# The last batch of a perceiver block, finished by tiles of 128 latents

## The chip, the cores and the metric

The kernel runs on one core of a Trainium2 chip. Its time is the device time of one execution in microseconds; for each kernel the median of several runs is given. A profile is one further execution, recorded by the hardware profiler; its row times are in microseconds from its first instruction.

The core's engines are TensorE (PE in the profile; PEld is its weight load), VectorE (DVE), ScalarE (ACT), GpSimd (POOL) and SyncE (SP, here only for DMAs). Each works off its own queue in order. PE writes to PSUM, eight banks of 2 KB per partition; DVE and ACT read it.

## What is computed

One perceiver layer on four batches of 256 latents with 256 channels; each batch has a context of 4096 rows with 192 channels. All in float32.

```python
x = x + xattn(layernorm(x), ctx)   # 16 heads of 16; 256 queries, 4096 keys
x = x + attn(layernorm(x))         # causal, 16 heads; q and k normed by head
x = x + ffn(layernorm(x))
# ffn: h = gelu([x, slot mean] @ w1 + b1); logits = h @ w2 + b2, scaled by tau
#      alpha = softmax over the 8 largest of 64 logits
#      slots = GRU(alpha.T @ x / sum(alpha), slot_init); slots mix by an attention
#      y = layernorm(slots + mixed); out = alpha @ (y @ wvp + bvp) @ wo + bo
```

## The kernel before

**Cross-attention.** The context comes in chunks of 512 keys (8 per batch). `keys` (L74) and `values` (L101) make a chunk's keys `kt` (channels first) and values `v`, with a column of ones beside each head, so that weighing also gives the softmax denominators. An iteration of the main loop (L2150 on) takes two blocks of 128 keys against all 256 latents. `cross_block` (L1769) does the scores of one block: 8 matmuls of 512 columns (`scores`, L161; two heads by 256 latents, on four row groups of PE), and the exps on ACT into `prob`. `cross_weigh` and `weigh` (L170) multiply the exps with the values: 8 matmuls per block and half of the heads, 256 columns, four column groups of PE. `cross_add` (L1790) adds the result from PSUM to `sums` on DVE. So 16 iterations make a batch, and four batches one long stream.

**Order.** PE, DVE and ACT run in the order of the program text; no scheduler moves their instructions. The eight banks are four pairs, turned by one step with each iteration (L2156). An iteration is: scores of the first block, weighing of the *iteration before* (`behind`), scores of the second block, then planned extra work (`take`), then keys (even iterations) or values (odd ones) of the next chunk, which the iterations after it use.

**The other layers** of batch b are cut into steps, put by `plan` (L1684 to L1760) into the iterations of batch b+1: `cross_turn`, `att_turned`, `cross_out` (the output of cross-attention), `x1_turned`, `qk`, `self_values`, `qk_turned` (the input of self-attention), an iteration of self-attention, `self_out`, `x2_turned`, `hidden`, and for the slots `routing`, `slot_inputs`, `alpha_turned`, `gates` and on. The slots of two batches (0 and 1, 2 and 3) go together. `first_more` and `second_more` (L1749, L1753) stand in the last two iterations of the last batch: the slot values of batches 0 and 1, routing, slot inputs and alpha of batch 2, and `give` (L1653) for batches 0 and 1: two matmuls of alpha with the slot values, `x2` added on DVE, DMA to the output.

**The ending** (`ending`, L1886) is what the last batch has left when the stream ends, with nothing to lie beside: weighing of the last two blocks, turning and dividing (`turn`, L189), `channels_turned`, `project` by `wo`, norm, `qk_product`, `self_values`, `head_sums` and `head_root`, `qk_turned`, self-attention with `last_block` (8 exps), masks on DVE (`self_masks`), `self_weigh`, `project` by `awo`, norm, `w1`, Gelu, `routing`, slots of batches 2 and 3, outputs. Each step takes all 256 latents (two tiles of 128, t = 0 and 1). `fill` (L1055) puts idle matmuls of 0.43 us into PE's waits. `preload` (L944) has ACT load a function table early. `moments`, `rsqrt` (L925: by ACT's root and a reciprocal, or by ten steps on DVE) and `all_in_range` (L1662, a check of the denominators) are on DVE. `temp()` (L918) gives one of 8 scratch buffers in turn.

Of the kernel before, what the change touches and what calls it, by code (L numbers as in the profile page):

```python
# [900 lines left out]
def fast_(es, tc, nc, a, out, k, const, x0):  # L901
# [219 lines left out]
    def same_rows(col):  # L1121

        t = small.tile([P, P], F32, name="same", tag="same")
        nc.vector.tensor_copy(t, col.to_broadcast([P, P]))
        return t
# [27 lines left out]
    def set_norms(bank):  # L1153

        rep = small.tile([P, P], F32, name="same", tag="same")
# [235 lines left out]
    def self_out(s, bank):  # L1391
        for t in range(QT):
            product(
                bank[:, t * C : (t + 1) * C],
                lambda c: s.attT[:, c, t * P : (t + 1) * P],
                lambda c: awo[:, c, :],
            )
        s.x2 = held.tile([P, QT, C], F32, name="x2", tag="x2", bufs=3)
        nc.vector.tensor_tensor(s.x2, halves(bank), s.xo, ALU.add)
        yield  # L1400
        apply = norm(s.x2)
        yield
        yield
        s.x2n = held.tile([P, QT, C], F32, name="x2n", tag="x2n", bufs=1)
        apply(s.x2n)
        with_bias(s, "x2", s.x2, fbo)
# [8 lines left out]

    def routing(s, bank):

        for t in range(QT):
            nc.tensor.matmul(
                bank[:, t * SLOTS : (t + 1) * SLOTS],  # L1420
                s.hT[:, t * P : (t + 1) * P],
                w2,
                start=True,
                stop=True,
            )
        lg, rest, best, ex = (
            small.tile([P, QT, n], F32, name=name, tag=name, bufs=1)
            for name, n in (("lg", SLOTS), ("rest", SLOTS), ("best", 8), ("ex", SLOTS))
        )
        top, asum = (small.tile([P, QT], F32, name=name, tag=name) for name in ("top", "asum"))  # L1430
# [6 lines left out]
        yield  # L1437
        for t in range(QT):
# [45 lines left out]
    def alpha_turned(s, bank):  # L1484
# [5 lines left out]
        if s.b % 2 == 0:  # L1490
            s.two.alphaT = held.tile([P, NQ], F32, name="alphaT", tag="alphaT", bufs=1)
        nc.scalar.copy(s.two.alphaT[r], bank[r, 0:NQ])

    def gates(w, *room):

        r, z, n, keep = (
            small.tile([P, 2, S2], F32, name=f"gate_{x}", tag=f"gate_{x}", bufs=1) for x in "rznk"
# [143 lines left out]
    def given(s, t, dst, start=True):  # L1641
# [3 lines left out]
            dst, s.two.alphaT[r, t * P : (t + 1) * P], s.two.sv[r], start=start, stop=True  # L1645
# [7 lines left out]
    def give(s, bank):  # L1653
# [3 lines left out]
        nc.vector.tensor_tensor(res, halves(bank), s.x2, ALU.add)  # L1657
# [88 lines left out]

    def first_more(x_0, x_1, y_0, y_1):  # L1749
        slot_values(batches[0].two, x_1)  # L1750
        return routing(batches[B - 2], x_0)

    def second_more(x_0, x_1, y_0, y_1):  # L1753
        s = batches[B - 2]
        slot_inputs(s, x_0)
        alpha_turned(s, x_1)
        for e, bank in zip(batches, (y_0, y_1)):
            give(e, bank)

    plan[B - 1, 15, 5], plan[B - 1, 16, 5] = first_more, second_more  # L1760
# [107 lines left out]
    def last_block(s, c, pairs):  # L1868

        pr = {}  # L1870
        for (j, h), sc in zip(((1, 0), (1, 1), (0, 0), (0, 1)), pairs):
            n = 2 * NQ // (j + 1)
            pt = pr[j, h] = pp.tile([P, 2, 2 * NQ], F32, name="prob", tag="prob")
            for m in range(2):
                r = pair_rows(h, m)
                nc.tensor.matmul(
                    sc[:, m, 0:n],
                    s.sk[r, c, j * P : (j + 1) * P],
                    s.sq[r, c, :, j * P :],
                    start=True,  # L1880
                    stop=True,
                )
            nc.scalar.activation(pt[:, :, 0:n], sc[:, :, 0:n], AF.Exp)
        return pr

    def ending(blocks, *pairs):  # L1886
# [3 lines left out]
        both_ = s.two  # L1890
        (x_0, x_1), (y_0, y_1), (z_0, z_1), (w_0, w_1) = ([m[:, i, :] for i in range(2)] for m in pairs)

# [4 lines left out]
        def channels_turned(bank, src, c):  # L1897
            for t in range(QT):
                nc.tensor.transpose(
                    bank[:, t * P : (t + 1) * P], src[:, t, c * P : (c + 1) * P], ident  # L1900
                )

        def tokens_turned(bank, src, t):
            for c in range(2):
                nc.tensor.transpose(
                    bank[:, c * P : (c + 1) * P], src[:, t, c * P : (c + 1) * P], ident
                )

        def tokens(dst, bank, t, copy):
            copy(  # L1910
                dst[:, :, t * P : (t + 1) * P],
                bank[:, 0:C].rearrange("p (c q) -> p c q", c=2),
            )

        def turn_half(sums, which, c, bank):
            return turn(nc, k, small, sums[c], c, bank, dens[:, s.b, which, c], s.att)

        def project(weights, banks_, alone):
            for c in range(2):
                for t in range(QT):  # L1920
                    nc.tensor.matmul(
                        banks_[t][:, 0:C],
                        s.attT[:, c, t * P : (t + 1) * P],
                        weights[:, c, :],
                        start=(c == 0 and alone),
                        stop=(c == 1),
                    )


        cross_weigh(s, blocks, 0, y_0)  # L1930
        cross_add(s, 0, y_0)
        preload(AF.Sqrt)
        cross_weigh(s, blocks, 1, y_1)


        s.att = halves(temp())
        divide = turn_half(s.sums, 0, 0, z_0)
        cross_add(s, 1, y_1)
        divide()
        turn_half(s.sums, 0, 1, z_1)()  # L1940
        s.attT = halves(temp())
        channels_turned(w_0, s.att, 0)
        nc.scalar.copy(s.attT[:, 0, :], w_0[:, 0:NQ])
        fill(x_1, 0.43)
        channels_turned(w_1, s.att, 1)
        nc.vector.tensor_copy(s.attT[:, 1, :], w_1[:, 0:NQ])
        project(wo, (x_0, y_1), True)
        for t, bank in enumerate((x_0, y_1)):
            nc.vector.tensor_tensor(s.xo[:, t, :], bank[:, 0:C], s.xo[:, t, :], ALU.add)


        s.x1T = halves(temp())
        tokens_turned(z_0, s.xo, 0)
        tokens(s.x1T, z_0, 0, nc.vector.tensor_copy)
        tokens_turned(z_1, s.xo, 1)
        tokens(s.x1T, z_1, 1, nc.scalar.copy)
        s.qk = held.tile([P, QT, 2 * C], F32, name="qk", tag="qk", bufs=1)
        s.var = small.tile([P, QT * 2 * H], F32, name="var", tag="var")
        rs = small.tile([P, QT * 2 * H], F32, name="rs_h", tag="rs_h")
        s.eps = small.tile([P, QT], F32, name="epsx", tag="epsx")  # L1960
        s.rs1 = small.tile([P, QT], F32, name="rs1", tag="rs1")

        def qk_product(t, bank):
            product(
                bank,
                lambda c: s.x1T[:, c, t * P : (t + 1) * P],
                lambda c: wqkv[:, c, 0 : 2 * C],
# [286 lines left out]
```

## Time and profile before

| what | value |
|---|---|
| median of 3 runs | 848.32 us (848.3 to 848.55) |
| the profiled execution | 850.1 us, of which span 848.2 us |
| granted TensorE clock, mean | 0.995 |
| busy | PE 828.2, ACT 605.7, DVE 309.1, POOL 16.7 us |
| last four iterations, start of the first block's scores | 741.61, 752.15, 762.77, 772.48 us |
| last weighing, start | 785.00 us |
| logits of the last batch on DVE | 821.24 us |
| last DMA issue | 842.09 us |

How to read it. A row of the timeline is: start, duration, engine, line, operation, written tile, read tiles, shapes and count; a bracket at its end gives the engine's idle time before it, and what ended it. The ends of matmuls are modelled, starts are recorded; a matmul in float32 leaves two records. "32*128" before a shape is the part of the array used, rows by columns: four such matmuls run beside each other. The chain is what ended last, followed back from the end; "issue" is time with no wait that the profile shows. Lines are those of the kernel of that profile. A stretch's row gives its length, busy time of each engine with the number of instructions, granted clock (1.00 is full), DMA share and GB/s.

### The profile page before, as it was taken

To read this page: it belongs to the slowest core of one execution; us is meant where nothing else is said; L and a number is where in the kernel's file an instruction comes from. 1 tells how busy PE (TensorE), PEld (TensorE's weight loads), DVE (VectorE), ACT (ScalarE), POOL (GpSimd) and SP (SyncE) were. 2 spreads that over 40 slices of the span, in tenths; PEclk is the share of its full clock that TensorE was granted. 3 is DMA by queue.
4 is the path that set the end of the run, shared out by engine and by line. 5 is a ranking of instruction groups with operands and counts; after the bars stand their busy time and mean duration, and the time that the engine had idled before them with its cause. 6 is when DMAs were issued, how large, how long until landed. Compare 5 with 4: busy or idle time off the path is not lost.

```text
span 848.2 us, 18509 instructions
## 1 busy us (share of the span) xinstructions
PE 828.2 (98%) x7975; PEld 440.2 (52%) x7975; DVE 309.1 (36%) x760; ACT 605.7 (71%) x842; POOL 16.7 (2%) x20
## 2 busy tenths in 40 slices
PE   8999999999999999999999999999999999999885
PEld 5445455545555555545545555555545555445554
DVE  3124234232263352212253453332334433123663
ACT  4777776767677768777677767767768767877551
POOL 1000100000000010000000010000000000000000
PEclk9999999999999999999999999999999999999998
DMA  7600101000000000000000000000000000000000
GB/s 204 163 27 26 26 14 63 26 27 26 26 26 26 2 26 26 26 26 27 27 26 26 2 26 26 26 25 2 26 26 26 26 19 10 24 2 2 26 1 29
DMA packets 21817, 25.79 MB, mean 30 GB/s; under 512 B 6240, under 2 KB 13280, under 8 KB 21728
## 3 DMA queue, kind: packets, MB, share of 16 engines
q1 hardware_dynamic: 20784, 23.75, 9.8%
q8 instruction: 64, 1.05, 0.5%
q10 hardware_dynamic: 848, 0.79, 0.3%
q14 instruction: 25, 0.20, 0.1%
q0 software_dynamic: 96, 0.01, 0.0%
HBM read 23.48 MB, written 1.05 MB: 29 GB/s over the span
## 4 chain that ended last, share of the span: by engine, by line
PE 94%; ACT 2%; DVE 2%; issue 0%; ACTq 0%; DVEq 0%
PE banks L165 30%; PE banks L179 27%; PE banks L993 7%; PE banks L80 7%; PE banks L107 7%; PE banks L86 4%; PE banks L120 4%; PE banks L1845 1%; PE banks L981 1%; PE banks L194 1%; PE banks L1058 1%; ACT prob L1782 1%; PE banks L1814 1%; PE banks L1461 1%; ACT prob L1824 0%
## 5 line engine op out<-in xcount | busy, mean ns | idle before, releaser
L1782 ACT ACTIVATE prob<-banks 128x1024 f32<-128x1024 f32 x384 | 366.8, 1045 | 0.0
L165 PE MATMUL banks<-qh,kt 32*128 32x512 f32 x2048 | 267.7, 620 | 1.5 <-DVE qh L1036 1.2
L179 PE MATMUL banks<-prob,v 128*32 128x256 f32 x4096 | 234.3, 381 | 1.6 <-DVE tmp L1657 0.8
L1780 ACT ACTIVATE prob<-banks 128x512 f32<-128x512 f32 x256 | 138.9, 595 | 130.8 <-PE banks L165 130.5
L179 PEld LDWEIGHTS banks<-prob,v 128*32 128x32 f32 x4096 | 126.5, 110 | 125.7 <-ACT prob L1780 45.8
L165 PEld LDWEIGHTS banks<-qh,kt 32*128 32x128 f32 x2048 | 103.9, 183 | 119.2 <-issue 66.9
L1796 DVE TENSOR_TENSOR sums<-banks,sums 128x512 f32<-128x512 f32 x120 | 82.6, 690 | 194.3 <-PE banks L179 168.5
L107 PE MATMUL banks<-wv,ctx 128*128 128x256 f32 x256 | 61.6, 384 | 0.0
L80 PE MATMUL banks<-ctx,wk 128*128 128x512 f32 x128 | 61.5, 603 | 0.1
L107 PEld LDWEIGHTS banks<-wv,ctx 128*128 128x128 f32 x256 | 46.8, 190 | 14.7 <-ACT prob L1780 7.6
L150 DVE COPY v<-banks 128x512 f32<-128x512 f32 x35 | 23.9, 690 | 81.4 <-PE banks L120 81.4
L94 DVE TENSOR_SCALAR kt<-banks,bk 128x512 f32<-128x512 f32 x32 | 24.0, 750 | 66.9 <-PE banks L86 66.8
L150 ACT COPY v<-banks 128x512 f32<-128x512 f32 x29 | 17.0, 586 | 30.1 <-PE banks L120 28.8
L120 PE MATMUL banks<-wv,ctx 64*128 64x256 f32 x256 | 36.3, 402 | 0.0
L86 PE MATMUL banks<-ctx,wk 64*128 64x512 f32 x128 | 36.1, 641 | 0.0
L95 ACT ACTIVATE kt<-banks,bk 128x512 f32<-128x512 f32 x32 | 22.1, 689 | 18.0 <-PE banks L86 17.1
L80 PEld LDWEIGHTS banks<-ctx,wk 128*128 128x128 f32 x128 | 20.9, 189 | 21.6 <-ACT prob L1782 12.1
L120 PEld LDWEIGHTS banks<-wv,ctx 64*128 64x128 f32 x256 | 22.0, 186 | 11.1 <-issue 9.3
L1829 DVE TENSOR_TENSOR prob<-prob,tri 128x512 f32<-128x512 f32 x32 | 20.8, 688 | 10.5 <-ACT prob L1824 9.8
L987 DVE COPY tmp<-banks 128x512 f32<-128x512 f32 x17 | 11.7, 691 | 33.8 <-PE banks L981 33.8
L1824 ACT ACTIVATE prob<-banks 128x512 f32<-128x512 f32 (+1 forms) x30 | 17.9, 694 | 8.5 <-PE banks L1814 8.5
L993 PE MATMUL banks<-wqkv,tmp 128*128 128x512 f32 (+1 forms) x64 | 23.0, 497 | 0.7 <-ACT prob L1824 0.5
(276 smaller groups left out, 504.9 us busy)
## 6 DMA issues: line engine op xcount, KB each, us to landing
ctx<-in_ctxT SPq DMA_DIRECT2D x32, 256.0 KB, 3.1
ctx<-in_ctxT SPq DMA_DIRECT2D x64, 128.0 KB, 3.2
x<-in_x SPq DMA_DIRECT2D x4, 256.0 KB, 3.5
wih<-in_ffn_WihT SPq DMA_DIRECT2D x1, 768.0 KB, 7.9
tmp<-in_ffn_WhhT SPq DMA_DIRECT2D x3, 256.0 KB, 5.8
out<-tmp SPq DMA_DIRECT2D x3, 256.0 KB, 2.3
wq<-in_L_xattn_Wq ACTq DMA_DIRECT2D x1, 256.0 KB, 5.8
wo<-in_L_xattn_Wo SPq DMA_DIRECT2D x1, 256.0 KB, 5.1
```

The lines of the kernel that those rows point to most:

```text
L80: nc.tensor.matmul(pk[c], k.wk[:, 0, c * P : (c + 1) * P], cx[:, 0, :], start=True, stop=False)
L86: nc.tensor.matmul(pk[c], k.wk[left(c), 1, c * P : (c + 1) * P], cx[left(c), 1, :], start=False, stop=True,)
L94: nc.vector.tensor_scalar(kt[:, 0, :], pk[0], k.bk[:, 0:1], None, ALU.add)
L107: nc.tensor.matmul(pv[n // 2][:, n % 2, :], cx[:, 0, n * P : (n + 1) * P], k.wv[:, 0, :], start=(n % 2 == 0), stop=False, skip_group_check ...
L120: nc.tensor.matmul(pv[u][:, i, :], cx[left(u), 1, n * P : (n + 1) * P], k.wv[left(u), 1, :], start=False, stop=True, skip_group_check=True,)
L150: copy(v[:, :, 0 : H * VW].rearrange("p i (h w) -> p i h w", w=VW)[:, :, :, 0:D], src.rearrange("p i (h d) -> p i h d", d=D),)
L165: nc.tensor.matmul(sc[:, m, :], kt[r, c, i * P : (i + 1) * P], qh[r, c, :], start=True, stop=True)
L179: nc.tensor.matmul(po[q * 32 : (q + 1) * 32, s * NQ : (s + 1) * NQ], v[:, i, w0 : w0 + 32], pr[s][:, m, e * NQ : (e + 1) * NQ], start=(fir ...
L993: nc.tensor.matmul(dst, lhs(c), rhs(c), start=(c == 0), stop=(c == 1))
L1780: nc.scalar.activation(pt[:, m, :], sc[:, m, :], AF.Exp)
L1782: nc.scalar.activation(pt, sc, AF.Exp)
L1796: nc.vector.tensor_tensor(s.sums[c], bank, s.sums[c], ALU.add)
```

## The change

The last batch goes by tiles of 128 latents in its last four iterations. They hold chunks 6 and 7. Before, each iteration took two blocks of keys for all latents; now the first two take chunks 6 and 7 (four blocks each) for the first tile, the other two the same chunks for the second. `tile_block`, `tile_weigh` and `tile_add` stand for `cross_block`, `cross_weigh` and `cross_add`. The last two iterations do the output of cross-attention for the first tile (`tile_out`) and its input to self-attention (`tile_in`), in place of `first_more` and `second_more`. In the ending, the self-attention of the first tile (keys of the first tile alone) goes beside the cross output of the second, then that of the second tile; further steps go tile by tile. Of what `second_more` did, `slot_inputs` of batch 2 is now in the ending behind the logits, and the outputs of batches 0 and 1 (`given_out`) stand beside the gates and behind `at_turned`; x2 is added by an identity matmul, and ACT copies. `all_in_range` moves behind the gates. Small buffers become scratch of `temp()`, and x2, x2n and alphaT have one buffer more.

The diff, cut to its core; `vec` is nc.vector, `act` nc.scalar:

```diff
+    def tile_block(s, n, t, kt, v, pairs):
+        q = s.qh.rearrange("p c (e q) -> p c e q", e=2)[:, :, :, t * P : (t + 1) * P]
+        for c in range(2):
+            for u in range(2):
+                for h in range(2):
+                    for m in range(2):
+                        r = pair_rows(h, m)
+                        nc.tensor.matmul(
+                            pairs[2 * c + h][:, m, u * NQ : (u + 1) * NQ],
+                            kt[r, c, (2 * n + u) * P : (2 * n + u + 1) * P],
+                            q[r, c],
...
+    def tile_weigh(blocks, c, bank):
+        for k_, (v_, n, pr) in enumerate(blocks):
+            for u in range(2):
+                for h in range(8):
...
+                        bank[h % 4 * 32 : (h % 4 + 1) * 32, g * P : (g + 1) * P],
+                        v_[:, 2 * n + u, w0 : w0 + 32],
+                        pr[c, g][:, m, u * NQ + e * P : u * NQ + (e + 1) * P],
...
-    def give(s, bank):
-        for t in range(QT):
-            given(s, t, bank[:, t * C : (t + 1) * C])
-        res = halves(temp())
-        nc.vector.tensor_tensor(res, halves(bank), s.x2, ALU.add)
+    def given_out(s, bank):
+        for t in range(QT):
+            to = bank[:, t * C : (t + 1) * C]
+            nc.tensor.matmul(
+                to, ident, s.x2[:, t, :], start=(t == 0), stop=False, skip_group_check=True
+            )
+        for t in range(QT):
+            given(s, t, bank[:, t * C : (t + 1) * C])
+        res = halves(temp())
+        nc.scalar.copy(res, halves(bank))
         send(s, slice(0, QT), res, nc.sync)
...
+    def tile_out(x_0, x_1, y_0, y_1):
...
+        for c in range(2):
+            tile_turn(tile_of(s.sums[c], 0), x_0, c)
+        put = tile_divide(s, x_0, (0, 1), 0, 0)
+        put(nc.vector.tensor_copy)
+        slot_values(batches[0].two, x_1)
+        tokens_turned(y_0, s.att, 0)
+        tokens(s.attT, y_0, 0, nc.vector.tensor_copy)
+        g = routing(d, y_1)
+        next(g)
+        project(s, wo, x_0, 0)
+        tile_residual(s, x_0, 0)
+        tile_variance(s, 0)
...
+    def tile_in(x_0, x_1, y_0, y_1):
...
+        tokens_turned(x_0, s.xo, 0)
+        tokens(s.x1T, x_0, 0, nc.vector.tensor_copy)
+        alpha_turned(d, y_1)
...
+        sq = tile_qk(s, 0, x_1)
+        tile_v(s, 0, y_0)
+        tile_heads(s, 0, sq)
+        heads_ = s.var_t[:, 0, 0 : 2 * H]
+        nc.vector.tensor_scalar(heads_, heads_, 1.0 / D, s.eps_t[:, 0:1], ALU.mult, ALU.add)
+        s.rs0 = rsqrt(s.var_t[:, 0, :])
+        tile_factors(s, 0, x_1, s.rs0[:, 0 : 2 * H])
...
     def ending(blocks, *pairs):
...
+        tile_weigh(blocks, 0, y_1)
+        tile_add(s, 0, y_1, 1)
+        tile_weigh(blocks, 1, x_0)
+        tile_add(s, 1, x_0, 1)
+        tile_qk_turned(s, 0, z_0, z_1, act, act, act)
+        tile_v_moved(s, 0, y_0, s.rs0[:, 2 * H :])
+        for c, bank in enumerate((w_0, w_1)):
+            tile_turn(tile_of(s.sums[c], 1), bank)
+        puts = [tile_divide(s, bank, (c,), 0, 1) for c, bank in enumerate((w_0, w_1))]
+        tokens_turned(y_1, s.att, 1)
+        tokens(s.attT, y_1, 1, vec.tensor_copy)
+        for put in puts:
+            put(vec.tensor_copy)
+        prs = first_scores(s, (z, w))
+        project(s, wo, x_0, 1)
+        tile_residual(s, x_0, 1)
         preload(AF.Sqrt)
+        tokens_turned(y_1, s.xo, 1)
+        tokens(s.x1T, y_1, 1, vec.tensor_copy)
+        tile_mask(prs[0].rearrange("p m (u q) -> p m u q", q=P))
+        tile_variance(s, 1)
+        sq = tile_qk(s, 1, x_1)
+        tile_mask(prs[1].rearrange("p m (u q) -> p m u q", q=P))
+        tile_v(s, 1, x_0)
...
+        tile_heads(s, 1, sq)
...
+        nc.vector.reciprocal(rs, rs)
+        tile_factors(s, 1, x_1, rs[:, 0 : 2 * H])
+        first_weigh(s, prs, z_0)
+        sums0 = as_sums(z_0, 4, act.copy)
         preload(AF.Exp)
         for c in range(2):
+            tile_turn(sums0[:, 2 * c : 2 * c + 2, :], z_1, c)
+        fill(w_0, 0.86)
+        tile_qk_turned(s, 1, y_0, y_1, vec, vec, act)
+        tile_v_moved(s, 1, x_0, rs[:, 2 * H :])
...
+        for j in range(2):
+            for h, pair in enumerate((x_, y)):
+                second_scores(s, 0, h, pair, j)
+        p0 = [second_exp(pair) for pair in (x_, y)]
...
+        for h, pair in enumerate((x_, y)):
+            for j in range(2):
+                second_scores(s, 1, h, pair, j)
+            p1.append(second_exp(pair))
+        project(s, awo, w_1, 0, alone=False)
+        second_mask(p0[1])
+        mv0 = tile_stats(w_1[:, 0:C])
...
+        with_abo(1)
+        second_weigh(s, p0, 0, z_0)
+        sums0 = as_sums(z_0, 2, vec.tensor_copy)
+        second_mask(p1[0])
...
+        second_mask(p1[1])
+        second_weigh(s, p1, 1, z_1)
+        sums1 = as_sums(z_1, 2, vec.tensor_copy)
...
+        logits(s, 0, x_0[:, 0:SLOTS])
+        fill(y_1, 0.43)
+        logits(s, 1, y_0[:, 0:SLOTS])
...
         next(route)
-        fill(x_1, 1.72)
+        slot_inputs(d, z_0, z_1)
+        fill(x_1, 0.86)
         finish(route)
         slot_inputs(s, y_1, w_0)
         alpha_turned(s, w_1)
         finish(gates(both_, x_1, z_1, y_0))
-        fill(x_0, 1.29)
+        check_range = all_in_range()
+        next(check_range)
+        given_out(batches[0], x_0)
         slot_qk(both_, y_1, w_0)()
...
         at_turned(both_, y_1)
+        given_out(batches[1], z_0)
         count_bad(y_0)
         mixed_channels_first(both_, w_0)
...
+            tiled = b == B - 1 and real >= 12 and not own
+            if tiled:
+                if real % 2 == 0:
+                    at = (kt, v) if real == 12 else at
+                    which = at
+                else:
+                    which = (kt2, vs[(n + 1) % 3]) if real == 13 else (kt, v)
+                tt = (real - 12) // 2
+                first = tile_block(s, 0, tt, *which, (w, x_, y, z))
...
-            take(5, x_[:, 0, :], x_[:, 1, :], y[:, 0, :], y[:, 1, :])
+            if tiled and real >= 14:
+                room = x_[:, 0, :], x_[:, 1, :], y[:, 0, :], y[:, 1, :]
+                take_one(tile_out if real == 14 else tile_in, *room)
```

`tile_divide` is a reciprocal and a multiplication on DVE, from the turned sums in PSUM, and returns the copy of the denominators (`put`). `tokens` copies turned channels back, `tile_heads` sums squares by head, `tile_factors` applies the roots, `as_sums` copies weighed values from PSUM, `second_exp` is one exp of 1024 columns, `second_mask` one mask of 512.

## Prediction

> **What bounds the kernel now.** I read the page first (busy shares, chain by engine), then the chain in order of time for the last 65 us, the timeline of the same stretch, and the sums by stretch.
>
> ```profile
> span 848.2 us, 18509 instructions
> PE 828.2 (98%) x7975; PEld 440.2 (52%) x7975; DVE 309.1 (36%) x760; ACT 605.7 (71%) x842; POOL 16.7 (2%) x20
> PE 94%; ACT 2%; DVE 2%; issue 0%; ACTq 0%; DVEq 0%
> ```
>
> Until 785 us TensorE (PE) is the bound: 98% busy, 94% of the chain. After that it is a chain of small steps, in which each engine waits for another. From the chain and, under it, the timeline:
>
> ```profile
> 785.00 3.71 PE banks L179 x64
> 788.70 0.02 issue
> 788.73 0.70 DVE sums L1796
> 789.43 0.04 issue
> 789.47 0.66 PE banks L194 x4
> ...
> 820.51 0.71 PE banks L1419 x4
> 821.22 0.02 issue
> 821.24 0.30 DVE lg L1431
> ```
> ```profile
> 753.13 0.31 PEld L165 LDWEIGHTS banks<-qh,kt 32*128 32x128 f32 x8 [0.60 <-DVE kt L94]
> ...
> 822.78 0.29 DVE L1448 SCALAR_TENSOR_TENSOR lg<-rest,ex 128x128 f32<-128x128 f32 x1 [0.27 <-ACT ex L1446]
> ...
> 836.94 0.52 PEld L1598 LDWEIGHTS banks<-atT,fv 128*128 128x128 f32 x4 [0.37 <-DVE nbad L1676]
> ```
>
> To be seen: from the last weighing (785.0) to the logits of the last batch (821.2) 36 us pass, and the change works there. The other three lines are waits of 0.60, 0.27 and 0.37 us, at the places where it adds work. The profiled execution took 850.1 us for its span of 848.2; the median of the runs is 848.32. I sum in the span's times and put the difference on the median.
>
> **The change, part by part.** "Lag" is after minus before at the same step, in the times of the profile of before. Hops are taken as measured there: two turns to the copy that reads them 0.44, copy to the next matmul 0.48, a 512-wide product to the step that reads it 2.02.
>
> *Half-width matmuls.* Four iterations get twice as many matmuls of half the width. [...] But the self-attention weighs with 128 columns already:
>
> ```profile
> L1845 PE MATMUL banks<-prob,vself 128*32 128x256 f32 x32 | 2.1, 382 | 0.0
> L1845 PE MATMUL banks<-prob,vself 128*32 128x128 f32 x32 | 1.2, 272 | 0.0
> ```
>
> Both rows are two runs of 16 records, four at a time. Less the tail of each run (0.16 us) that is 0.22 and 0.11 us for four: half the width, half the time. [...] Scores of 256 columns keep pace likewise (0.216 us for four records in the self-attention).
>
> *Keys used one iteration earlier.* The first tile needs chunk 7 in the second tiled iteration (start 752.15), right behind its key product. The wait above shows when: DVE has moved these keys at 753.07, PE goes on at 753.13. Before, half of the block's scores lay ahead of this wait, and it ended at 754.0; now all 1.73 us of it come behind: 754.88. PE is the bound here and nothing gives it back: **+0.85**. If the copy were early it would be 0.
>
> *First tile's output, third tiled iteration (tile_out).* On PE: four turns, slot_values, two turns, logits, a project, before the next scores. The turns start at 770.3, divide and turns give att transposed at 772.2, its copy (behind sv on DVE) runs to 772.75, project 772.81 to 773.69. Before, PE waited until 773.39 for the last exp's bank. With the bank order in tile_block the weighing starts at 775.58 for 775.31: **+0.27** (it goes through to the next scores, 779.17). Gone: two batches' outputs, four matmuls each, and 0.84 us of PE's wait for DVE ahead of the last weighing.
>
> *First tile's qkv, fourth iteration (tile_in).* alpha_turned writes y_1 and waits for the exp of y (782.34); the 512-wide product behind it on PE starts at 782.84, Square at 784.87. DVE: reduce 785.5, scale, ten rsqrt steps (33 wide, taken at 0.225 between the 2-wide 0.2 and the 64-wide 0.26), factors to 789.4. Behind these on DVE stand the last tile_adds, though PE has weighed by 788.94: turns of c=1 at 790.18 for 789.47, **lag 0.7**.
>
> *Second tile's cross output.* Divides on DVE, turns 791.48, copy 791.82. On PE first_scores stand ahead of project, and their second pair of banks waits for the puts on DVE (792.5); scores end 793.4, project, residual to 794.87; before 793.56: **lag 1.3**.
>
> *Its qkv.* One 512-wide product (794.97 turns, 795.89 product, Square to 798.5) where there were two. But DVE has the masks of the first tile: two of 1024 wide, 1.35 us each (0.688 for 512, L1829), and reduce starts at 799.3, not 798.55. Min, root, reciprocal, factors end at 801.64; before 801.60: **lag 0**. Then PE does the first tile's turns (they wait for ACT's copy behind the root, 801.2) and two fills (0.86) before qk turned: 802.58. Moves by DVE (0.54 each) and v's by ACT: scores at 804.25 for 802.74, **lag 1.5**.
>
> *Its self-attention.* Four exps of 1.05 instead of eight (5.85 us). Banks serialize them: 805.27, 806.23, 807.45, 808.45 to 809.5. DVE takes mv0, abo and sums0 between the masks (project of tile 0 ends 809.1 on PE), so the last mask ends at 812.0, not 810.2. Weigh, copy, turn, divide, turn, copy (ACT), project by halves: statistics at 815.37, second tile before 816.09: **lag -0.7**.
>
> *FFN up to logits.* Root, norm, turns, Gelu by tiles; the table loads of 1.28 keep their place. Second Gelu ends 819.7 for 820.71, logits biased by 820.45 for 821.53: **lag -1.1**.
>
> *slot_inputs of batch 2, moved here.* PE's part lies in its wait. DVE gets 0.23 + 0.55 + 0.29 us between match_replace and the weighting of exps, queued ahead of the latter: it starts at 822.57 for 822.78, though its exps are ready by 821.7. The wait of 0.27 shown above is all the cover there was: **lag -0.2**.
>
> *Outputs of batches 0 and 1.* Each is two identity matmuls and two of alpha, 4 records of 0.216 each: 1.73 us on PE, one ACT copy (0.58) and a DMA on SP. The first replaces 1.29 us of fills (830.3 to 831.9) and ends at 832.1, before snT at 832.71: 0; without that cover 1.7. The second stands in front of mixed_channels_first, in a wait of 0.37 us: PE goes on at 838.4 for 836.94, **+1.45**. ACT has its copy done (839.0) before the root it needs. Both DMAs leave SP before the last send and land in 2.3 us (out rows): 0, else up to 2.
>
> *check_range* moves behind the gates: three DVE steps, 1.0 us, in a DVE wait of 1.18: 0. More buffers and scratch from tmp: no instruction and no wait shows; 0, ends 0 and 0.5.
>
> Sum: 0.85 - 0.2 + 1.45 = **+2.1**. The waits for two engines at once that the new order has in some ten places (a semaphore step of 0.05 us on PE) I take at +0.4 (0 to 1.2). So span 850.7, **median 850.8**.
>
> **Rivals.** *First tile's work is free* (faster). If all of it falls into waits of the second tile's chain, the second's scores start about 3.6 us sooner (tile_add at 789.1 instead of 789.7, no scores ahead of project 1.9, masks 0.7, fills 0.8; smaller overlaps), and DVE's order in the self-attention costs 1.7 less: 850.8 - 5.3 = 845.5. For it: DVE is busy only 7.5 of 10.0 us and PE is idle by turns there. Against: queues are in order, and the waits are shorter than the pieces. It decides if the second tile's scores start less than 13 us after the last weighing ends (I say 15.3).
>
> *Half of that is free:* 848.2. Same mechanism, the change then does its work and gives it back in given_out and the key wait.
>
> *The clock gate closes once more* (slower still). The stretches:
>
> ```profile
> 799.05:802.46 3.41, 2.19 (x13) 1.40 (x11) 2.95 (x7) 2.83 (x7) 0.00 (x0) 1.00 0.00 0
> ...
> 822.94:826.36 3.42, 2.44 (x20) 2.16 (x20) 1.94 (x7) 0.22 (x1) 0.00 (x0) 1.00 0.00 0
> 826.36:829.77 3.41, 3.41 (x19) 3.41 (x18) 1.38 (x4) 0.56 (x2) 0.00 (x0) 0.50 0.00 0
> ```
>
> The columns after the length are PE, PEld, DVE, ACT, POOL, granted clock, DMA. After a thin stretch the clock is 0.50, and the gates' 24 records take 4.57 us, which at 0.109 each are 2.6. [...] In the new tail the stretch before the second tile's scores is as thin (0.87 + 0.44 + some fill, of 3.4). Half clock over fills, turns and scores: +2, 852.8.
>
> **Chances.** Forecast 0.55 (849.5 to 852.0), gate 0.17 (to 854), free 0.18, half 0.10. Two runs differ little, and about 0.2% (1.7 us) is what a measurement of this kernel tells from no change. Faster: the free case, 0.18. Same (to 850.0): the half case and a fifth of the forecast, 0.20. Slower 0.62. Range 846.0 to 853.8: most of the free case and the worst of the gate are left out.
>
> **What would show it.** Right: a PE wait for kt of about 1 us in the second tiled iteration; mask rows 1024 wide on DVE ahead of the reduce; PE in given_out when atT is ready, mixed_channels_first 1.5 us later; 32x128 weighings at 0.11 us for four. Wrong: the second tile's scores under 13 us behind the last weighing, a clock of 0.50 in other stretches, DVE idle before its masks.

## The result, and the profile after

| | before | after |
|---|---|---|
| median, runs | 848.55 us, 9 | 851.76 us, 9 (850.88 to 852.38) |
| ratio, 95% interval | | 1.0032 (1.0023 to 1.0041) |
| profiled execution, its span | 850.1, 848.2 us | 850.88, 849.1 us |
| granted clock, mean | 0.995 | 0.998 |

The change makes the kernel slower by 0.32%, 3.2 us; 850.8 was predicted, with a range of 846.0 to 853.8. The page after:

```profile
span 849.1 us, 19377 instructions
PE 826.4 (97%) x8403; PEld 451.4 (53%) x8403; DVE 307.3 (36%) x776; ACT 606.0 (71%) x841; POOL 16.8 (2%) x20
PE 93%; DVE 3%; ACT 2%; issue 1%; DVEq 0%; ACTq 0%
```

TensorE is busy for 826.4 us, before for 828.2, but it has about as much to do: that execution of before did its gates at half clock, and the profile of `b1_before_more_fill` (below), with 0.86 us more of idle matmuls and full clock in the gates, has 827.0. More of the chain is on the vector engine and in waits.

The spans differ by only 0.9 us where the medians differ by 3.2, because the profiled execution of before was one of its longer ones: its gates ran at half clock (1.13 us, by `b1_before_more_fill`), and it came 1.09 us later to its last four iterations (the key product of chunk 7: 749.18 and 748.09). 0.9 + 1.13 + 1.09 is 3.1. So from here on every time is counted from that key product, and before is taken without its half clock. The *distance* from the key product to the end is 97.87 us before (in the profile of `b1_before_more_fill`) and 100.97 us after: +3.10. The end is the last semaphore step of the vector engine, 0.03 us before the span's end; the last output's DMA lies ahead of it.

The rows for the keys of chunk 7, from the timeline of before:

```profile
749.18 1.98 PE L80 MATMUL banks<-ctx,wk 128*128 128x512 f32 x4
...
752.15 2.12 PE L165 MATMUL banks<-qh,kt 32*128 32x512 f32 x16
754.20 3.66 PE L179 MATMUL banks<-prob,v 128*32 128x256 f32 x64
757.79 2.06 PE L165 MATMUL banks<-qh,kt 32*128 32x512 f32 x16
```

And the rows of after that answer to those shown of before (a bracket is the idle time ahead and what ended it):

```profile
748.09 1.99 PE L80 MATMUL banks<-ctx,wk 128*128 128x512 f32 x4
...
752.13 2.01 PE L1876 MATMUL banks<-qh,kt 32*128 32x256 f32 x32 [1.00 <-DVE kt L94]
754.07 3.70 PE L1900 MATMUL banks<-prob,v 128*32 128x128 f32 x128
...
786.19 3.70 PE L1900 MATMUL banks<-prob,v 128*32 128x128 f32 x128
...
804.51 1.15 PE L2098 MATMUL banks<-sq,sk 32*128 32x256 f32 x16 [1.02 <-DVE rect L1934]
...
823.17 0.28 DVE L1448 SCALAR_TENSOR_TENSOR lg<-tmp 128x128 f32<-128x128 f32 x1
...
835.64 1.03 PE L1664 MATMUL banks<-x,ident 128*128 128x256 f32 x4
836.60 1.13 PE L1646 MATMUL banks<-sv,alphaT 64*128 64x256 f32 x4
837.66 0.19 PE L1688 MATMUL banks<-ones,least 128*1 128x1 f32 x2
837.78 0.71 PE L1600 MATMUL banks<-atT,fv 128*128 128x128 f32 x4
```

To be seen: TensorE stands 1.00 us for the keys of chunk 7. Before, only its weight load (PEld) stood, for 0.60 us, while the matmuls still had half of a block's scores to do: these scores took 2.12 us, 0.06 more than those of the next block. A weighing of 128 half-width records takes 3.70 us; before, 64 full ones took 3.66. The weighting of the exps (L1448) no longer has an idle time ahead: its engine was busy with `slot_inputs`. And L1600 (mixed_channels_first) has `given_out` ahead of it (L1664, L1646), though its input was ready at 836.14.

The lag at each step, counted from the key product, against the recorded steps (there with the 0.85 of the keys added from the first row on):

| step | lag forecast | lag measured | growth forecast / measured |
|---|---|---|---|
| weighing behind the key wait | 0.85 | 0.96 | +0.85 / +0.96 |
| weighing of the 4th iteration (tile_out) | 1.12 | 1.70 | +0.27 / +0.74 |
| turns behind the last weighing (tile_in) | 1.55 | 2.2 | +0.43 / +0.5 |
| residual of the second tile, end | 2.15 | 3.20 | +0.6 / +1.0 |
| its factors, end | 0.85 | 1.62 | -1.3 / -1.58 |
| its scores | 2.35 | 2.86 | +1.5 / +1.24 |
| its statistics | 0.15 | 1.13 | -2.2 / -1.73 |
| logits biased | -0.25 | 0.82 | -0.4 / -0.31 |
| weighting of the exps | 0.65 | 1.48 | +0.9 / +0.66 |
| snT, end of the gates | 0.65 | 1.48 | 0 / 0 |
| mixed_channels_first | 2.1 | 3.07 | +1.45 / +1.59 |
| last step | 2.5 | 3.10 | +0.4 / +0.03 |

The nine executions of the changed kernel lie up to 1.5 us apart, so gains of tenths are read from the distance in the profile, one for each kernel, and the medians are given beside it. The distance repeats well: up to the step that an edit touches, the profiles of the edited kernels agree with that of the changed kernel within 0.03 us. From the last operation of the vector engine to the end they take 6.12 to 6.25 us, so the distance is good to about 0.1 us. The edited kernels were timed later than the changed one, each beside the kernel before, whose medians there were 848.23 to 848.47.

### The profile page after: what moved, and what is told of

The parts are those of the page before. It is cut to its first block, busy times and chain, and to the rows that moved or that the text cites. A ratio compares the mean times of both kernels' runs of the same rounds, so it can differ in the third digit from the quotient of the medians.

```text
span 849.1 us, 19377 instructions
## 1 busy us (share of the span) xinstructions
PE 826.4 (97%) x8403; PEld 451.4 (53%) x8403; DVE 307.3 (36%) x776; ACT 606.0 (71%) x841; POOL 16.8 (2%) x20
## 4 chain that ended last, share of the span: by engine, by line
PE 93%; DVE 3%; ACT 2%; issue 1%; DVEq 0%; ACTq 0%
PE banks L165 28%; PE banks L179 25%; PE banks L993 7%; PE banks L80 7%; PE banks L107 7%; PE banks L86 4%; PE banks L120 4%; PE banks L1876 2%; PE banks L1900 1%; PE banks L981 1%; PE banks L1843 1%; PE banks L1058 1%; PE banks L1812 1%; PE banks L194 1%; ACT prob L1780 1%; PE banks L1461 1%
## 5 line engine op out<-in xcount | busy, mean ns | idle before, releaser
L165 PE MATMUL banks<-qh,kt 32*128 32x512 f32 x1920 | 250.2, 620 | 1.2 <-DVE qh L1036 1.2
L179 PE MATMUL banks<-prob,v 128*32 128x256 f32 x3840 | 219.6, 381 | 0.8 <-ACT prob L1822 0.5
L1778 ACT ACTIVATE prob<-banks 128x512 f32<-128x512 f32 x240 | 130.3, 595 | 121.7 <-PE banks L165 121.4
L179 PEld LDWEIGHTS banks<-prob,v 128*32 128x32 f32 x3840 | 118.6, 110 | 117.0 <-ACT prob L1778 42.8
L165 PEld LDWEIGHTS banks<-qh,kt 32*128 32x128 f32 x1920 | 97.6, 183 | 111.1 <-issue 62.5
L1794 DVE TENSOR_TENSOR sums<-banks,sums 128x512 f32<-128x512 f32 x112 | 77.1, 691 | 178.4 <-PE banks L179 155.8
L993 PE MATMUL banks<-wqkv,tmp 128*128 128x256 f32 (+1 forms) x56 | 19.6, 482 | 0.5 <-ACT prob L1822 0.5
```

What stands on the lines that cost most here:

```text
L165: nc.tensor.matmul(sc[:, m, :], kt[r, c, i * P : (i + 1) * P], qh[r, c, :], start=True, stop=True)
L179: nc.tensor.matmul(po[q * 32 : (q + 1) * 32, s * NQ : (s + 1) * NQ], v[:, i, w0 : w0 + 32], pr[s][:, m, e * NQ : (e + 1) * NQ], start=(fir ...
L993: nc.tensor.matmul(dst, lhs(c), rhs(c), start=(c == 0), stop=(c == 1))
L1778: nc.scalar.activation(pt[:, m, :], sc[:, m, :], AF.Exp)
L1794: nc.vector.tensor_tensor(s.sums[c], bank, s.sums[c], ALU.add)
```

## The experiments

My theory was that the 3.1 us are three terms (the keys one iteration earlier, `slot_inputs` on the vector engine, batch 1's output on TensorE), while the tile-by-tile ending gives back only what it costs. The rivals: the ending itself loses, or the clock does. Edits are on the changed kernel unless it says otherwise.

**`b1_before_more_fill`**: the kernel before, `fill(x_1, 1.72)` made `fill(x_1, 2.58)`.

> The kernel before with two more idle fills (0.86 us) in the wait of TensorE that ends 0.98 us later with alpha of the last batch. It asks what the profiled execution of the kernel before had of its own: 850.1 us against a median of 848.5, with half clock in the gates. My theory (after the thin stretch at 823 to 826 us the clock is halved in some executions, not in all; where it is, 1.1 us are lost): with this cover the half clock behind 823 us is gone in all runs, the higher times (850 and above) become fewer or vanish, and the median is 848.0 to 848.5. Rival (the higher times come from the start of the span, where the clock opens later in some executions): half clock behind 823 us is gone, and the times still lie in two groups 1 to 2 us apart. Rival (the fills delay alpha's sums): all times higher by 0.3 to 0.9 us.

Measured: 848.31 us (14 runs) against 848.47 (28 runs of before). Of before, 9 of the 28 executions took 849.75 to 850.56 with a mean clock of 0.995; with the fill one of 14 did (850.43, 0.995). In all sets of before together it is 48 of 140. The stretches around the gates, with more fill (columns: PE, PEld, DVE, ACT, POOL busy, granted clock, DMA share, GB/s):

```profile
822.12:825.53 3.41, 3.29 (x23) 2.66 (x21) 2.10 (x7) 0.24 (x1) 0.00 (x0) 1.00 0.00 0
825.53:828.95 3.42, 3.42 (x29) 3.26 (x28) 1.59 (x5) 0.78 (x2) 0.00 (x0) 1.00 0.00 0
```

The stretch ahead of the gates is 3.29 us busy, not 2.44, and the clock stays at 1.00. Up to alpha both profiles agree within 0.01 us; the gates end 1.13 us sooner. So the half clock of the profile of before belongs to about a third of its executions, and its price is 1.13 us. The prediction had not taken it out.

**`e3_keys_by_half`**

```diff
-        nc.vector.tensor_scalar(kt[:, 0, :], pk[0], ...)
-        nc.scalar.activation(kt[:, 1, :], pk[1], ...)
+        for a_ in (slice(0, 256), slice(256, 512)):    # chunk 7 alone
+            nc.vector.tensor_scalar(kt[:, 0, a_], pk[0][:, a_], ...)
+            nc.scalar.activation(kt[:, 1, a_], pk[1][:, a_], ...)
```

> One edit on the changed kernel: the two copies of the last chunk's keys out of their banks, 512 wide each, are made in two halves of 256 each, the keys of the first two blocks first. My theory (TensorE stands 1.0 us for these copies at the second tiled iteration, and nothing gives that back): the wait falls from 1.00 to about 0.65 us, all that follows moves by 0.3 to 0.4 us, and the time falls by as much, to 851.4. Rival (the wait is given back later, in the wait for the last exps' banks at 770 to 774 us): the wait falls, and the last weighing starts at the same time as before the edit; within 0.1 us.

Measured: 850.90 us (13 runs). The wait is 0.73 us for 1.00, and the distance 100.68 for 100.97: all of the 0.27 arrives at the end. TensorE is the bound there, and nothing gave the wait back.

**`e1_output_in_fill`** and **`f1_copy_behind_exps`**

```diff
         slot_inputs(d, z_0, z_1)
-        fill(x_1, 0.86)
+        given_out(batches[1], x_1)          # e1: with its copy
+        moved = given_out(batches[1], x_1, True)   # f1: matmuls alone
         finish(route)
+        moved()                             # f1: copy and DMA
...
         at_turned(both_, y_1)
-        given_out(batches[1], z_0)
```

> One edit on the changed kernel: the output of batch 1 (its second place, between the turn of the mixing weights and mixed_channels_first) goes where two idle fills stand, behind slot_inputs of batch 2. My theory (its 1.73 us on TensorE stand on the path there, with only some 0.4 us of wait before): mixed_channels_first starts 1.5 us sooner against the start of the gates, TensorE in the new place still waits for alpha (2.1 us of fill and wait before, 1.73 used), and the time falls by 1.4 to 1.6 us, to 850.3. Rival (the output is hidden by the vector engine's and ScalarE's chain, and the loss is elsewhere): within 0.4 us of 851.8. Rival (the new place delays alpha's sums by what it does on TensorE or ScalarE): the gates start over 0.5 us later and less than 1.0 us is gained.

> The same move of batch 1's output as in e1_output_in_fill, but ScalarE's copy of it is now queued behind the exps of the last batch's routing, not ahead of them. There the copy waited for TensorE until 824.6, and the exps, their table load and alpha behind it came 4.2 us late. My theory (the output costs 1.58 us in its place in the changed kernel, and nothing in the wait for alpha if no queue is blocked): weighting of the exps starts where it does in the changed kernel, mixed_channels_first comes 1.6 us sooner than there against snT, the time falls by 1.4 to 1.7 us, to 850.2. Rival (the clock is what counts, and the long output only moves the thin stretch): half clock appears behind 825 us in most runs and less than 0.8 us is gained.

Measured: e1 855.90 us (6 runs, one at 861.58), 4 us slower; f1 849.94 (22 runs), 1.8 faster than the changed kernel. The timeline of e1 shows why:

```profile
824.62 0.58 ACT L1670 COPY tmp<-banks 128x512 f32<-128x512 f32 x1 [3.84 <-PE banks L1646]
825.23 1.28 ACT L1446 ACT_TABLE_LOAD   x1
...
826.52 0.59 ACT L1446 ACTIVATE tmp<-lg,top 128x64 f32<-128x64 f32 x2
827.14 0.29 DVE L1448 SCALAR_TENSOR_TENSOR lg<-tmp 128x128 f32<-128x128 f32 x1 [3.62 <-ACT tmp L1446]
```

ScalarE stood 3.84 us for the output's last matmul, and the exps with their table load stood behind it in the queue; the weighting came 3.7 us later than in the changed kernel (not the 4.2 of the second expectation). TensorE was busy for 0.29 us of the 3.41 from 825.2 on, and what followed was slow: L1461's last 8 records took 1.91 us, the gates' 24 4.63 (1.06 and 2.94 in the changed kernel; 4.57 for the 24 at half clock in before), at a mean clock of 0.993 for 0.998. My own first edit had overlooked the copy: of a step that is moved, every instruction counts. In f1 the exps go first, the weighting starts where it does in the changed kernel (within 0.03 us), and mixed_channels_first starts right behind its input:

```profile
837.09 0.71 PE L1600 MATMUL banks<-atT,fv 128*128 128x128 f32 x4 [0.26 <-DVE nbad L1693]
```

From the end of snT to it are 4.2 us for 5.8, in e1 too. The distance is 99.50 (-1.47), so the term is real, and in the wait for alpha the output is free to within 0.1 us.

**`f4_slot_inputs_early`**

```diff
+        slot_inputs(d, y_1, w_1)
         gelu0 = hidden_product(0, x_1)
-        fill(y_1, 0.43)
...
-        slot_inputs(d, z_0, z_1)
-        fill(x_1, 0.86)
+        fill(x_1, 2.15)
```

> One edit on the changed kernel: slot_inputs of batch 2 goes ahead of the hidden layer's product of the first tile, in the wait of TensorE at 816.3 to 817.5 and that of the vector engine at 818.0 to 818.9; two idle fills are dropped there, and three more put where it was. My theory (its 1.07 us on the vector engine delay the weighting of the exps by 0.7 us, for the exps are done at 822.4 and the weighting starts at 823.17): weighting starts right behind the exps, and the logits come 0.1 to 0.3 us later; the time falls by 0.4 to 0.6 us, to 851.3. Rival (the logits are delayed as much as is won, since the vector engine's copy of the turned norm stands behind it): within 0.2 us.

Measured: 850.37 us (22 runs); distance 100.38 (-0.59). The weighting waits for the exps again, and follows them:

```profile
822.28 0.59 ACT L1446 ACTIVATE tmp<-lg,top 128x64 f32<-128x64 f32 x2
822.90 0.29 DVE L1448 SCALAR_TENSOR_TENSOR lg<-tmp 128x128 f32<-128x128 f32 x1 [0.34 <-ACT tmp L1446]
```

**`u1_three_terms_undone`**: e3, f4 and f1 together, with one idle matmul of 0.43 us left beside the output.

> The changed kernel with the three terms of my sum undone or cut at once: keys by halves (as e3), slot_inputs of batch 2 ahead of the hidden layer (as f4), batch 1's output in the wait for alpha with its copy behind the exps (as f1). From the key product of chunk 7 to the last step on the vector engine the changed kernel takes 100.97 us, the kernel before (without the half clock) 97.87. If the terms add up (0.29, 0.59 and 1.47 as measured one by one), it takes 98.6 us and the time is 849.2 to 849.6: the first tile ahead gains nothing by itself. Rival (the three share one cover): over 99.2 us, above 850. Rival (they were all of it, and the tiles gain): under 97.9, under 848.5.

Measured: distance 98.51 (98.6 expected); 848.83 us (13 runs), ratio to before 0.9998 (0.9990 to 1.0006). The three terms add up, and without them the kernel is as fast as before, though not faster: the ending by tiles gains nothing by itself. What is left of the lag, 98.51 - 97.87 = 0.64, is about as much as the rest of the key wait (0.96 - 0.29 = 0.67); no edit took that rest away.

**`e2_no_fill`**: `fill(w_0, 0.86)` ahead of the second tile's turns is gone.

> One edit on the changed kernel: the two idle fills (0.86 us) behind the turns of the first tile's self-attention sums are gone. My theory (they stand on the path: the factors of the second tile's queries and keys are ready at 802.13, TensorE turns them at 802.89): the second tile's scores come 0.7 us sooner and the time falls by 0.6 to 0.8 us, to 851.1. Rival (they keep the clock up in a stretch in which TensorE is busy under 70%): a row of half clock appears after 800 us and the time rises by 1 to 2 us. Rival (the second tile's scores wait for something else, the copies of v or the divide): within 0.2 us.

Measured: 851.56 us (8 runs, 849.93 to 853.18). Both happen. The second tile's scores come 0.66 us sooner; and the clock halves later in most executions (mean clock 0.996 or less in six of eight; the two at 0.998 took 849.93 and 850.81). In the profiled one:

```profile
809.97:813.38 3.41, 2.99 (x39) 1.59 (x39) 2.72 (x8) 0.54 (x3) 0.00 (x0) 1.00 0.02 7
813.38:816.79 3.41, 1.92 (x10) 1.19 (x10) 2.16 (x8) 1.65 (x6) 0.00 (x0) 1.00 0.00 0
816.79:820.21 3.42, 2.90 (x12) 2.22 (x12) 0.78 (x4) 1.63 (x3) 1.27 (x1) 0.50 0.00 0
820.21:823.62 3.41, 3.41 (x16) 3.23 (x16) 1.56 (x11) 2.24 (x4) 0.00 (x0) 0.50 0.00 0
823.62:827.03 3.41, 3.41 (x14) 2.84 (x14) 1.62 (x6) 0.00 (x0) 0.00 (x0) 0.50 0.00 0
```

Three stretches at 0.50, and the distance is 103.50, 3.2 us more than the 100.3 that the sooner scores would make. The changed kernel has a stretch as thin at the same place, and keeps its clock in this execution:

```profile
814.37:817.78 3.41, 1.91 (x10) 1.21 (x10) 2.17 (x8) 1.66 (x6) 0.00 (x0) 1.00 0.00 0
821.20:824.61 3.41, 2.31 (x17) 1.86 (x16) 2.80 (x15) 1.20 (x3) 0.00 (x0) 1.00 0.00 0
```

So the two fills did not guard the place where they stand. Taking them out shifted the rest, and the half clock came from 816.79 on, some 14 us behind them. Busy time alone does not decide here: behind 1.91 us (the changed kernel) the clock stays at 1.00, behind 1.92 (e2) and 2.44 (before) it goes to 0.50. What decides is open.

**`f2_masks_first`** and **`f5_masks_and_bias_first`**: the vector engine's order in the second tile's self-attention.

```diff
         tokens(s.attT, w_0, 0, vec.tensor_copy)
+        with_abo(1)                         # f5 alone
...
         second_mask(p0[1])
+        second_mask(p1[0])
+        second_mask(p1[1])
-        mv0 = tile_stats(w_1[:, 0:C])       # f5: behind sums0
...
-        with_abo(1)                         # f5 alone
         second_weigh(s, p0, 0, z_0)
         sums0 = as_sums(z_0, 2, vec.tensor_copy)
-        second_mask(p1[0])
...
-        second_mask(p1[1])
         second_weigh(s, p1, 1, z_1)
```

> One edit on the changed kernel: on the vector engine the last two masks of the second tile's self-attention come ahead of the first tile's statistics, residual bias and the copy of the first sums, not behind. My theory (the order on this queue is what holds the self-attention of the second tile: its last mask ends at 812.6, though its exp is done at 809.9): the last mask ends at 810.6 to 810.9, the second weighing and the copy of its sums come 1.1 to 1.4 us sooner, and so do the logits and the end: 850.5. Rival (the first tile's statistics are then late, and its hidden layer holds the logits): less than 0.5 us. Rival (an earlier chain only brings a longer wait at Gelu's table load): less than 0.3 us.

> As f2_masks_first, and mended: there TensorE stood until 811.86 in the residual of the second tile (an identity matmul queued between the two weighings) for the bias that the vector engine adds behind the masks, and nothing was gained. Now this bias is added ahead of the masks, and the copy of the first sums stands ahead of the first tile's statistics. My theory (what was late next in f2 was this one wait): the last mask ends at about 810.7, both weighings run behind each other, the copy of the second sums starts 1.1 to 1.3 us sooner than in the changed kernel (813.16), and logits and end come 0.9 to 1.3 us sooner: 850.8. Rival (the first tile's statistics, root and norm, now later, hold the hidden layer): under 0.4 us.

Measured: f2 851.83 us (7 runs), distance 101.26 (+0.29); f5 850.31 (12 runs), distance 100.34 (-0.63). The timeline of f2:

```profile
810.03 0.69 DVE L2053 TENSOR_TENSOR prob<-prob,tri 128x512 f32<-128x512 f32 x1 [0.22 <-ACT prob L2108]
...
811.86 0.70 PE L2192 MATMUL banks<-xo,ident 128*128 128x256 f32 x2 [0.85 <-DVE xo L2188]
812.49 1.08 PE L2119 MATMUL banks<-prob,vself 128*32 128x128 f32 x32
```

The last mask is done at 810.72 as I wanted, but the second weighing stands behind a residual on TensorE that waits for a bias now queued behind the masks. One wait took the place of the other. With the bias ahead (f5) the weighings follow each other and 0.63 us arrive, less than my 0.9 to 1.3: with the masks out of the way TensorE does weighing, residual and weighing without a wait between them, and the copy of the second sums follows. Of f5's 12 runs four had clocks of 0.988 to 0.996 and took 852.3 to 856.0; f3 (below) has four such of 19, e3 two of 13, and f1 one at 857.86.

**`f3_project_between`**

```diff
-        prs = first_scores(s, (z, w))
+        scores = first_scores(s, (z, w))    # by pair, a generator
+        prs = [next(scores)]
         project(s, wo, x_0, 1)
         tile_residual(s, x_0, 1)
-        preload(AF.Sqrt)
+        next(scores)
         tokens_turned(y_1, s.xo, 1)
+        prs.append(next(scores))
+        preload(AF.Sqrt)
```

> One edit on the changed kernel: the first tile's scores go pair of banks by pair, and the second tile's project goes between them; its turn goes ahead of the last four scores. My theory (the first tile's scores, 1.8 us, stand on the path ahead of project): residual of the second tile starts 1.0 us sooner (795.25 before), its norm's reduce 0.8 us sooner, limited by the second mask on the vector engine, and the second tile's scores 0.5 to 0.9 us sooner: 851.1. Rival (ScalarE's table load or the copies of the first tile hold the second tile's scores): reduce sooner, scores at the same time, within 0.2 us. Rival (thin stretch at 793 to 797 us becomes thinner, the clock halves): slower by over 1 us.

Measured: 850.65 us (19 runs); distance 100.38 (-0.59). The residual comes 0.74 us sooner, the reduce 0.54, and all of that arrives. What is late next is two things at once: Square, which waits for the table load that the second, now later, exp pushed back, ends at 799.73, and the second mask at 799.69, and the reduce needs both.

**`g1_all`** and **`g2_all_no_fill`**

> All edits that gained, in one kernel: keys by halves, alpha_turned of batch 2 behind the first tile's products, scores of the first tile with project between them, the masks and the bias ahead of the statistics, slot_inputs of batch 2 in the hidden layer's wait, batch 1's output in the wait for alpha; the two fills ahead of the turns of the second tile's queries and keys stand behind them, and the second tile's scores go to the banks that those fills used and not to those that hold v. If the gains add up: 100.97 less 0.29, 0.4, 0.59, 1.1, 0.59, 1.47 and 1.0 is 95.5 us from the key product to the last step (97.87 in the kernel before), and the time 845.8 to 846.6, faster than both. Rival (the edits free the same waits twice): 96.5 to 97.9, no faster than before by more than 0.2%. Rival (the clock halves in the shorter waits): over 848.

> As g1_all, without the two fills at the second tile's scores. By the order of the queues they cost nothing where they stand in g1_all (TensorE waits there for copies by the vector engine and ScalarE): same time within 0.3 us. Rival (what e2_no_fill showed: without them TensorE does too little in a stretch of 3.4 us, and the clock halves behind 815 us in most executions): 1 to 3 us slower than g1_all, with a row of half clock.

Measured: g1 847.54 us (18 runs), ratio 0.9984 (0.9977 to 0.9991); g2 847.11 (13 runs), ratio 0.9977 (0.9969 to 0.9985), so 0.23% faster than before and by the medians 0.55% faster than the change. The distances are 96.65 in g2, and in g1 97.94, of which I put 1.3 down to half clock in its profiled execution (mean clock 0.995, for 0.999 in g2's; up to the end of the gates both profiles agree within 0.02 us). I had expected 95.5: `alpha_turned` behind the products gained nothing (the last addition to the sums stands at the same place as in e3), the masks brought 0.63 of 1.1, fill and banks 0.7 of 1.0 (the remainder of the sum). Leaving the fills out cost nothing here, against the rival: mean clocks of 0.996 or less are in 3 of 13 runs of g2 and in 8 of 18 of g1. That `slot_inputs` and the output now fill the thin stretches is a likely reason, not a tested one.

## Why the prediction was right, and where it was not

**Right in direction and mechanism.** Slower, by the terms named, each at its place. The half-width matmuls cost what the rows of the self-attention said, +0.04 us a weighing (3.70 for 3.66, 0.16 in four). Key wait: +0.85 said, +0.96 measured, and e3 shows that it is not given back. `given_out` of batch 1: +1.45 said, +1.59 measured, -1.47 when moved (f1). That of batch 0 and `check_range` are hidden, as said: the lag of snT equals that of the weighting, and with batch 1's output moved (f1) it is 4.2 us from snT to mixed_channels_first, as before. `slot_inputs`: +0.9 said, +0.66 measured, -0.59 when moved (f4).

**Mis-sized: the ending up to the logits.** I had it gain 1.1 us; it gained 0.14 (0.82 less the 0.96 of the keys). The terms: tile_out +0.74 for +0.27 (0.15 is lost ahead of the turns, in the third iteration's first scores, 2.18 us for 2.06, and its weighing; 0.1 at att's copy behind sv; and project holds TensorE 1.07 us until the next scores, not 0.88); the second tile's cross output +1.0 for +0.6; the self-attention -1.73 for -2.2. Each was in the list, with its cause; I took each hop at its shortest. The +0.4 that I had set aside for waits on two engines was spent here, not at the end. That the whole is only 0.6 short is in part luck: this allowance and a `slot_inputs` that came 0.24 cheaper cover two thirds of the 0.96 by which the ending was mis-sized.

**The base.** I put the sum on 848.32 by the difference of the profiled execution. The execution was one with half clock and a late start, which the sums by step cancel, so this did no harm to the forecast (the gates' 24 records take 2.94 us at full clock, as after shows, not the 2.6 that it took them for). Nor did it harm that the 0.60 us shown for the keys was the weight load's wait, since the sum counts when TensorE goes on. The base itself was 848.55 in nine runs. Forecast lag 2.5, measured 3.1 (profile) and 3.2 (medians).

**The rivals.** *First tile's work is free*: the second tile's scores start 14.6 us behind the end of the last weighing (15.3 said, under 13 would have been this case). False, for the reason given: the queues are in order (in e1 the weighting of the exps came 3.7 us later, because a copy ahead of the exps in ScalarE's queue stood for 3.84). A part of it can be had by changing the order: 0.59 us in f3, 0.63 in f5, and 1.86 from u1 to g2, which has both and other places for fills and banks. That is far from the 5.3 that this rival was about. *Half clock once more*, the slower rival: false for this kernel's profile (1.00 in all stretches of the ending) and for eight of nine runs by the mean clock (0.998, the ninth 0.996), but near: by mean clocks of 0.996 or less e2 has it in six of eight runs and f5 in four of twelve. My reading, that a thin stretch is enough, was too simple: it rested on one row of before (2.44 us of 3.41 busy, then 0.50), and e2 has another (1.92), but stretches of 1.91 and 2.31 us keep the clock at 1.00 in the changed kernel.

Left open: five of the nine runs of after have spans of 850.0 to 850.5 us and four 849.1 to 849.4, with the same mean clock but in one, and the profile of after is one of the four. That fits with the medians of the edited kernels being lower against after's median by 0.2 to 0.8 us more than their distances say. A different start of the span (last section) could make such a difference; with one profile of this kernel it is not shown. Open too is on which property of a stretch half clock follows.

## What to carry to other kernels

A moved step is a PE part, a copy and a DMA in three queues; put each where its own queue waits, and look what stands behind it there (e1 and f1 differ in the place of one copy, and by 6 us, half clock included). Where an engine is the bound, look for a wait to be paid in full at the end (e3: 0.27 of 0.27 us); where a chain is, an edit is paid by whatever is next late, so edit, look for the next wait, and edit again (f2 +0.29 us, f5 -0.63). Before summing on a profiled execution, look whether its clock and its start are those of the median run.

## What the runs showed of the hardware

The granted clock went to 0.50 behind stretches in which TensorE was busy 1.92 of 3.41 us (e2) and 2.44 (before), and stayed at 1.00 behind others of 1.91 and 2.31 (the changed kernel) and 2.19 (before, 799.05 to 802.46). It stayed at 0.50 for 3.41 us in before (826.36 to 829.77) and for 10.24 in e2 (816.79 to 827.03), and cost 1.13 and 3.2 us there. With 0.86 us of idle matmuls added to the one of before (2.44 made 3.29, `b1_before_more_fill`), one of 14 runs had a mean clock of 0.995, for 9 of 28 without. These are single executions and stretches; what sets the clock they do not show.

The start of a span moves the whole: the 16 idle matmuls ahead of all other work of TensorE take 6.51 us in the profile of before and 5.64 in that of after, the first turn behind them starts at 7.83 and 6.97, and the key product of chunk 7 at 749.18 and 748.09. In the profiles of e2 and e3, whose kernels are alike up to there with the changed one, it starts at 747.78 and 748.15.
